# A conditioned attention layer with a routed feed-forward: two transposes of the attention stage moved from TensorE to VectorE's 32x32 blocks and transfers through memory

## The chip, the core and the metric

The kernel runs on one core of a Trainium2 chip. All data are fp32. The metric is the device time in microseconds of one execution. Three runs of the kernel before the change took 779.1, 781.33 and 787.7 us; the median, 781.33 us, is the time before. One more execution was profiled; the profile describes that one.

## What is computed

There are 16 sequences `x[b]` of 128 tokens, 256 wide, and for each a context of 128 tokens. Cut to what matters:

```python
z   = layernorm(layernorm(x)) * ln2_w + ln2_b
lat = z * (1 + cond) + cond                          # modulated, per sequence
kv_in = concat(layernorm(ctx) * ln1_w + ln1_b, lat)  # 256 tokens
q = lat @ Wq.T ;  k, v = split(kv_in @ Wkv.T)        # 16 heads of 64
x = x + (softmax(q @ k.T / 8) @ v) @ Wo.T
h = layernorm(x)                                     # "normed stream"
scores = h @ router                                  # 8 experts, the best one per token
x = x + shared_ffn(h) + routed_ffn(h, best expert)
```

Three places matter here. The two inputs of the attention, `ctx` and `x`, are normalised with tokens on partitions, and the projections need them with the 256 features on partitions: `kvT`. The result `h` of the second normalisation has tokens on partitions too, and the router and the shared feed-forward need it turned: `hT`. Both turns are what the change moves.

## The kernel before

Work goes in eight groups `g` of two sequences, b0 = 2g and b1 = 2g + 1. Attention runs in 32 **steps** `u`: one step is one sequence and half of its 16 heads, so a group has four: 2b0, 2b0+1, 2b1, 2b1+1. The order on every engine is the order in which the Python code emits instructions (a manual schedule), so each engine's queue is in program order, and a tile that is not yet free or not yet filled holds up all that is queued behind it.

`step(u, units, side, loads)` emits, in this order:

- `logits(u)` (L485): 8 products into two PSUM tiles `S`; then `keep_heads(u-2)` (L561, VectorE copies the heads of an earlier step out of PSUM);
- `maxima` of the first half (L497, VectorE), `exponents` of the first half (L504, ScalarE, 4 instructions), `maxima` of the second half;
- one **unit** from the list `units`; the `loads`; `normalise(u, 0)` (L514 a reciprocal on VectorE, L517 four multiplications on GpSimd); `exponents` of the second half;
- one unit; `normalise(u, 1)`; the first four of the `side` functions; one unit; the rest of `side`; all remaining units but one;
- `turn(u, n)` for both halves (L526: VectorE transposes 32x32 blocks of the probabilities into `px`; L530: SyncE's queue writes them to memory, `p_blocks`), `fetch(u)` (L538: SyncE's queue reads them back as `pT`, with keys on partitions); the last unit; `weigh(u-1)` (L550: probabilities times values for the step before).

A unit is a piece of TensorE work with the copy that takes its result out of PSUM: `k_unit` (L433, copied by ScalarE L441), `v_unit` (L452, copied by ScalarE L459), `q_unit` (L418, ScalarE L425), `finish` (L566, added to `xres` by VectorE L570), a piece of the shared feed-forward `hidden` (L149; SiLU on ScalarE L164, product on VectorE L165, in the last group only), and the two turns. All units share three PSUM buffers (`ps_m`, tag "mm"): a unit can start when the one three before it has been copied out. `S` has two buffers, `O` one.

The turns before the change:

- `inputs(g)`: statistics of four tiles (L314, L315), their variances (L320, L323), an inverse root by three Newton steps on tiny tiles (`newton`, L111 to L122), four normalisations in place or into `z` (L127); all as `side` of step 2b0+1, two groups ahead. Then `transpose([c])` for each half `c` of the features: four TensorE transposes against `ident` (L346, L347), and three VectorE instructions that apply weight and modulation while copying from PSUM into `kvT` (L348, L358). Half 0 is a unit of step 2b1, half 1 the first unit of the next group's step 2b0.
- `moe_inputs(g)`: the same for `h` of the group before: `x_rows` is written to memory (L581), statistics (L587, L588), variances (L593), its own Newton steps, normalisation and the write of `h_rows` (L604), as `side` of step 2b1; then in step 2b1+1 the unit `transpose` (L614: four TensorE transposes, L616: one VectorE copy into `hT`), and later the unit `choose` (L622: router products; L629).

The context tile `ctx` has one buffer, `xres` four, `kvT` two. `mwork` holds the tags "mid" (two buffers) and "xr" (three), which before the change only the feed-forward uses. After the last group come the rest of the shared feed-forward, the routing and 20 expert tiles; the change leaves them alone but for the place of one `choose`.

Of the kernel before, what the change touches and what calls it, by code (L numbers as in the profile page):

```python
# [9 lines left out]
F32 = mybir.dt.float32  # L10
# [7 lines left out]
P = 128  # L18
# [6 lines left out]
def resampler_attn__then__top1_moe_kernel(  # L25
# [100 lines left out]
    def normed(o, i, mr):  # L126
        nc.vector.tensor_scalar(o, i, mr[0], mr[1], ALU.subtract, ALU.mult)  # L127
# [118 lines left out]
    with ExitStack() as at:  # L246
# [53 lines left out]
        def inputs(g):  # L300

            st = {}

            def stats(i):
                if i == 0:
                    st["mv"] = small.tile([P, 4, 2], F32, tag="inmv", name=f"inmv_{g}")  # L310
                for k in (2 * i, 2 * i + 1):
                    t = (xres[g] if i == 0 else tokens[g])[:, k % 2, :]
                    s6 = small.tile([P, 6], F32, tag="inst", name=f"inst_{g}_{k}")
                    nc.vector.bn_stats(s6, t)  # L314
                    nc.vector.bn_aggr(st["mv"][:, k, :], s6)  # L315

            def variances():
                mv = st["mv"]
                v = small.tile([P, 4], F32, tag="inv", name=f"inv_{g}")
                nc.vector.tensor_scalar(  # L320
                    v[:, 0:2], mv[:, 0:2, 1], 1.0 + EPS, EPS * EPS, ALU.mult, ALU.add
                )
                nc.vector.tensor_scalar(v[:, 2:4], mv[:, 2:4, 1], EPS, None, ALU.add)  # L323
                st["newton"] = newton(small, v, 4, "in")

            def iterate(n):
                for _ in range(n):
                    st["r"] = next(st["newton"])

            def scale(i):  # L330
                if i == 0:
                    st["z"] = work.tile([P, 2, D], F32, tag="z", name=f"z_{g}", bufs=1)
                for k in (2 * i, 2 * i + 1):
                    t = (xres[g] if i == 0 else tokens[g])[:, k % 2, :]
                    o = (st["z"] if i == 0 else tokens[g])[:, k % 2, :]
                    normed(o, t, (st["mv"][:, k, 0:1], st["r"][:, k : k + 1]))

            def transpose(chunks):
                cs, z = tokens[g], st["z"]
                if chunks[0] == 0:  # L340
                    kvTs[g] = work.tile([P, DC, 2, 2, S], F32, tag="kvT", name=f"kvT_{g}")
                kvT = kvTs[g]
                for c in chunks:
                    pt = ps_m.tile([P, 2, 2, S], F32, tag="mm", name=f"kvt_{g}_{c}")
                    for i in range(2):
                        nc.tensor.transpose(pt[:, i, 0, :], cs[:, i, ts(c, P)], ident)  # L346
                        nc.tensor.transpose(pt[:, i, 1, :], z[:, i, ts(c, P)], ident)  # L347
                    nc.vector.tensor_scalar(  # L348
                        kvT[:, c, :, 0, :],
                        pt[:, :, 0, :],  # L350
                        vec[:, c, C_W1 : C_W1 + 1],
                        vec[:, c, C_B1 : C_B1 + 1],
                        ALU.mult,
                        ALU.add,
                    )
                    for i in range(2):
                        b = 2 * g + i
                        nc.vector.tensor_scalar(  # L358
                            kvT[:, c, i, 1, :],
                            pt[:, i, 1, :],  # L360
                            mod_w[:, c, b : b + 1],
                            mod_b[:, c, b : b + 1],
                            ALU.mult,
                            ALU.add,
                        )

            return (
                [lambda: stats(0), lambda: stats(1), variances]
                + [lambda: iterate(1)] * 3
                + [lambda: scale(0), lambda: scale(1)],  # L370
                transpose,
            )

        def first_inputs(i):
# [11 lines left out]
            nc.vector.tensor_scalar(  # L386
                v[:, 1:2], mv[:, 1, 1:2], 1.0 + EPS, EPS * EPS, ALU.mult, ALU.add
            )
            for r in newton(small, v, 2, "f"):
                pass  # L390
            z = work.tile([P, 2, D], F32, tag="z", name=f"fz_{i}", bufs=1)
            for k, t in enumerate(pair):
# [179 lines left out]
        def moe_inputs(g):  # L572

            b0 = 2 * g
            xr = xres[g]
            st = {}

            def stats():
                rows = slice(b0 * S, (b0 + 2) * S)
                keep_rows = s_rows if g == NG - 1 else x_rows  # L580
                nc.sync.dma_start(  # L581
                    out=keep_rows[rows, :].rearrange("(b p) d -> p b d", p=P), in_=xr
                )
                mv = small.tile([P, 2, 2], F32, tag="hmv", name=f"hmv_{g}")
                for i in range(2):
                    s6 = small.tile([P, 6], F32, tag="hst", name=f"hst_{g}_{i}")
                    nc.vector.bn_stats(s6, xr[:, i, :])  # L587
                    nc.vector.bn_aggr(mv[:, i, :], s6)  # L588
                st["mv"] = mv

            def variances():
                v = small.tile([P, 2], F32, tag="hv", name=f"hv_{g}")
                nc.vector.tensor_scalar(v, st["mv"][:, :, 1], EPS, None, ALU.add)  # L593
                st["newton"] = newton(small, v, 2, "h")

            def iterate():
                st["r"] = next(st["newton"])
# [1 line left out]
            def scale():  # L599
                st["h"] = work.tile([P, 2, D], F32, tag="h", name=f"h_{g}", bufs=1)  # L600
                for i in range(2):
                    normed(st["h"][:, i, :], xr[:, i, :], (st["mv"][:, i, 0:1], st["r"][:, i : i + 1]))
                rows = slice(b0 * S, (b0 + 2) * S)
                nc.sync.dma_start(  # L604
                    out=h_rows[rows, :].rearrange("(b p) d -> p b d", p=P), in_=st["h"]
                )
                xres.pop(g)
# [22 lines left out]

            return [stats, variances] + [iterate] * 3 + [scale], transpose, choose

        def step(u, units, side, loads=()):

# [2 lines left out]
            def aside(n):  # L639
                for f in side[:n]:  # L640
                    f()
                del side[:n]
# [18 lines left out]
            exponents(u, 1, ps[1], nm)  # L661
            unit()
            normalise(u, 1)
            aside(4)
            unit()
            aside(len(side))
            while len(units) > 1:
# [1 line left out]
            turn(u, 0)  # L669
            turn(u, 1)  # L670
            fetch(u)
            unit()
            if u > 0:
                weigh(u - 1)
# [17 lines left out]
            transpose(range(DC))  # L692
            load_tokens(2)

        late, in_rest = [], []
        for g in range(NG):
            b0, b1 = 2 * g, 2 * g + 1
            more = g + 1 < NG
            loads = [lambda: load_tokens(g + 2)] if 0 < g < NG - 2 else []
            q = [lambda j=j: q_unit(g + 1, j) for j in range(4)]  # L700
            k1 = [lambda j=j: k_unit(b1, j) for j in range(4)]
            v1 = [lambda j=j: v_unit(b1, j) for j in range(4)]
            k2 = [lambda j=j: k_unit(b1 + 1, j) for j in range(4)]
            v2 = [lambda j=j: v_unit(b1 + 1, j) for j in range(4)]
            wo_before = [lambda: finish(b0 - 1)] if g else []
            wo_first = [lambda: finish(b0)]
            if g > 0:
                late, h_transpose, choose = moe_inputs(g - 1)
                h_units = [h_transpose, choose]
            else:  # L710
                h_units = []
            new, in_transpose = inputs(g + 2) if g + 2 < NG else ([], None)
            if more:
                if g == 0:
                    step(0, k1 + [second_inputs] + q[:2], [])
                    load_shared()
                    v1 = [lambda j=j: v_unit(0, j) for j in range(1, 4)] + v1
                else:
                    step(2 * b0, in_rest + k1 + q[:2], [], loads)
                step(2 * b0 + 1, v1[:2] + wo_before + v1[2:], new)  # L720
                in_first = [lambda: in_transpose([0])] if in_transpose else []
                in_rest = [lambda f=in_transpose: f([1])] if in_transpose else []
                step(2 * b1, k2 + in_first + q[2:], late)
                step(2 * b1 + 1, v2[:1] + h_units[:1] + v2[1:2] + wo_first + h_units[1:] + v2[2:], [])
            else:

                sh = [shared_unit]
                step(2 * b0, k1 + sh * 2, [])
                step(2 * b0 + 1, wo_before + sh * 5, [])
                step(2 * b1, v1 + sh * 2, late)  # L730
                step(2 * b1 + 1, wo_first + sh + h_units[:1] + sh + h_units[1:] + sh, [])
        keep_heads(2 * B - 2)
        for j in range(NP // 2):
            shared_unit()
# [2 lines left out]
        keep_heads(2 * B - 1)  # L737
        shared_unit()
        finish(B - 1)
        late, h_transpose, choose = moe_inputs(NG - 1)  # L740
        for i, f in enumerate(late):
            f()
            if i % 2 == 1:
                shared_unit()
        shared_unit()
        h_transpose()
        shared_unit()
        choose()


    wexp = ctx.enter_context(tc.tile_pool(name="wexp", bufs=1))
# [425 lines left out]
```

## Time and profile before

| | |
|---|---|
| three runs | 779.1, 781.33, 787.7 us; median 781.33 |
| profiled execution, its own time | 778.67 us |
| span of its instructions | 776.8 us |
| granted TensorE clock | 1.0 |
| attention steps 2b0 to 2b1+1 of one middle group (S of 149.10 to S of 209.78) | 60.68 us |
| busy: TensorE, VectorE, ScalarE, GpSimd | 757.4, 412.6, 259.3, 313.0 us |
| mean DMA rate | 154 GB/s, 84,788 packets |

The span runs from the first to the last instruction of the program; the execution's own time is 1.9 us longer. In a line of the timeline the first number is the start in us from the span's start, the second the length, then engine, line, operation, written and read tiles; a bracket at the end says how long the engine had been idle and who released it. In a group line "x64 | 75.2, 1215" means 64 instructions, 75.2 us busy, 1215 ns each.

### The profile page before, as it was taken

Reading aid. Unit: us, or ns where it says so; the run is one execution under the profiler, and the core shown is the slowest. Engines: PE = TensorE matmul, PEld = TensorE weight load, DVE = VectorE, ACT = ScalarE, POOL = GpSimd, SP = SyncE. Lnnn points to the kernel's source line nnn. Section 1 sums busy time; section 2 is a strip of 40 time slices with the busy share of each in tenths; the row PEclk is TensorE's granted clock in tenths of the full one; section 3 lists DMA queues with packets and bytes.
Section 4 is the critical chain, followed back from the end, with each engine's and each line's share of the span. In section 5 each row is a group of like instructions: output and inputs, shape, how many; then the busy total and the mean of one; then the engine's idle time right before and its main releaser. Section 6 shows DMA issues by size and latency. Waiting matters only on the chain.

```text
span 776.8 us, 12221 instructions
## 1 busy us (share of the span) xinstructions
PE 757.4 (98%) x4156; PEld 587.0 (76%) x4156; DVE 412.6 (53%) x1000; ACT 259.3 (33%) x779; POOL 313.0 (40%) x366
## 2 busy tenths in 40 slices
PE   5999999999999999999999999999999999999997
PEld 4758768678677677687686777788888777787887
DVE  4475458558647647656744645635632354444532
ACT  2444533444354354344344455611311011010111
POOL 1363553464355345435544644521011234434331
PEclk9999999999999999999999999999999999999999
DMA  8075434633543553454345334532997334333332
GB/s 285 1 233 198 155 109 164 213 113 136 202 151 122 182 185 123 150 190 137 135 165 173 124 139 168 182 136 76 364 352 257 84 94 111 96 101 97 97 88 60
DMA packets 84788, 119.45 MB, mean 154 GB/s; under 512 B 10160, under 2 KB 68531, under 8 KB 84724
## 3 DMA queue, kind: packets, MB, share of 16 engines
q1 hardware_dynamic: 73380, 99.55, 37.8%
q0 software_dynamic: 4528, 13.18, 5.6%
q10 hardware_dynamic: 6816, 5.89, 2.5%
q8 instruction: 36, 0.59, 0.3%
q14 instruction: 28, 0.23, 0.1%
HBM read 68.78 MB, written 42.47 MB: 143 GB/s over the span
## 4 chain that ended last, share of the span: by engine, by line
PE 71%; DVE 15%; ACT 7%; issue 2%; DMA 2%; SPq 1%; POOL 0%; ACTq 0%; DVEq 0%; POOLq 0%
PE u L997 12%; PE pk L433 10%; PE pv L452 8%; PE p L149 8%; ACT pe L504 6%; PE yr L1046 6%; PE O L550 5%; PE pw L566 5%; PE S L485 5%; PE pq L418 5%; PE ys L179 5%; DVE px L526 3%; DVE nmx L497 2%; DVE ha L119 1%; DMA out_dram<-sg,table 1%
## 5 line engine op out<-in xcount | busy, mean ns | idle before, releaser
L517 POOL TENSOR_SCALAR pe<-pe,rs 128x256 f32<-128x256 f32 x256 | 230.9, 921 | 262.4 <-DVE rs L514 262.4
L504 ACT ACTIVATE pe<-S,nmx 128x256 f32<-128x256 f32 x256 | 118.4, 488 | 127.1 <-DVE nmx L497 127.1
L452 PE MATMUL pv<-wv,kvT 128*128 128x512 f32 x256 | 117.8, 601 | 0.2 <-ACT kT L441 0.2
L433 PE MATMUL pk<-kvT,wk 128*128 128x256 f32 x512 | 116.2, 386 | 0.4 <-DVE kvT L403 0.4
L433 PEld LDWEIGHTS pk<-kvT,wk 128*128 128x128 f32 x512 | 97.5, 193 | 16.7 <-issue 3.0
L526 DVE STREAM_TRANSPOSE px<-pe 128x512 f32<-128x512 f32 x128 | 81.4, 683 | 34.4 <-POOL pe L517 34.4
L997 PE MATMUL u<-w13s,xT 128*128 x320 | 98.0, 459 | 0.0
L452 PEld LDWEIGHTS pv<-wv,kvT 128*128 128x128 f32 x256 | 46.4, 190 | 50.3 <-issue 48.7
L997 PEld LDWEIGHTS u<-w13s,xT 128*128 128x128 f32 x320 | 59.4, 190 | 29.7
L497 DVE TENSOR_REDUCE nmx<-S 128x4 f32<-128x1024 f32 x64 | 75.2, 1215 | 12.3 <-PE S L485 12.3
L149 PE MATMUL p<-hT,ws 128*128 128x256 f32 x320 | 73.2, 381 | 0.5 <-DVE mid L165 0.5
L550 PEld LDWEIGHTS O<-pT,v 128*64 128x64 f32 x1024 | 55.2, 137 | 16.6 <-issue 14.6
L149 PEld LDWEIGHTS p<-hT,ws 128*128 128x128 f32 x320 | 60.1, 190 | 9.0 <-DVE mid L165 0.7
L485 PE MATMUL S<-kT,qT 64*128 64x256 f32 x512 | 63.9, 389 | 0.0
L1007 ACT ACTIVATE rsl<-u 128x352 f32<-128x352 f32 x40 | 18.4, 463 | 136.3 <-issue 67.8
L550 PE MATMUL O<-pT,v 128*64 128x128 f32 x1024 | 63.0, 276 | 0.0
L459 ACT COPY v<-pv 128x512 f32<-128x512 f32 x64 | 38.3, 599 | 73.0 <-PE pv L452 73.0
L566 PE MATMUL pw<-wo,oT 128*128 128x256 f32 x256 | 58.6, 382 | 4.0 <-ACT v L459 4.0
L566 PEld LDWEIGHTS pw<-wo,oT 128*128 128x128 f32 x256 | 48.1, 190 | 18.5 <-ACT v L459 9.8
L1008 DVE TENSOR_TENSOR body<-u,rsl 128x352 f32<-128x352 f32 x40 | 20.7, 524 | 74.1 <-issue 51.7
L418 PE MATMUL pq<-kvT,wq 128*128 128x256 f32 x256 | 58.1, 380 | 1.3 <-DVE kvT L358 1.3
L1046 PEld LDWEIGHTS yr<-wds,mT 128*128 128x128 f32 (+1 forms) x240 | 56.6, 309 | 2.0
(174 smaller groups left out, 810.6 us busy)
## 6 DMA issues: line engine op xcount, KB each, us to landing
p_blocks<-px SPq DMA_DIRECT2D x64, 512.0 KB
pT<-p_blocks SPq DMA_DIRECT2D x64, 512.0 KB
w13s<-in_w_dram SPq DMA_DIRECT2D x16, 704.0 KB
mT<-body SPq DMA_DIRECT2D x220, 24.0 KB
wds<-in_w_dram SPq DMA_DIRECT2D x8, 512.0 KB
mT<-body ACTq DMA_DIRECT2D x100, 24.0 KB
h_rows<-h SPq DMA_DIRECT2D x8, 256.0 KB
xres<-in_x_dram SPq DMA_DIRECT2D x7, 256.0 KB
```

The source lines that it names most:

```text
L149: nc.tensor.matmul(ps, lhsT=shared["w13"][:, c, ds(col, P)], rhs=hT[:, c, ts(t, TB)], start=(c == 0), stop=(c == DC - 1),)
L418: nc.tensor.matmul(pq[:, jj], lhsT=wq[:, c, ts(2 * j + jj, P)], rhs=kvTs[g][:, c, :, 1, :], start=(c == 0), stop=(c == DC - 1),)
L433: nc.tensor.matmul(pk[:, jj, :], lhsT=wk[:, c, ts(2 * j + jj, P)], rhs=kvTs[b // 2][:, c, b % 2].rearrange("p t s -> p (t s)"), start=(c = ...
L452: nc.tensor.matmul(pv, lhsT=kvTs[b // 2][:, c, b % 2, t, :], rhs=wv[:, c, ts(n, 512)], start=(c == 0), stop=(c == DC - 1),)
L485: nc.tensor.matmul(pl[:, r, j, :], lhsT=qTs[b // 2][rows, k, b % 2, :], rhs=kTs[b][rows, k, :], start=True, stop=True,)
L504: nc.scalar.activation(pes[u][:, h, :], pl[:, r, j, :], AF.Exp, bias=nmx[:, r, j : j + 1], accum_out=sums[u][:, h : h + 1],)
L517: nc.gpsimd.tensor_scalar(w, w, rs[:, i : i + 1], None, ALU.mult)
L526: nc.vector.transpose(px[:, :, t].rearrange("p j h q -> p h j q"), pes[u][:, ts(n, 4), ts(t, S)].rearrange("p h (j k) -> p h j k", k=BL),)
L550: nc.tensor.matmul(o[r * HD : (r + 1) * HD, j, :], lhsT=vs[b][:, t, ts(2 * (4 * half + j) + r, HD)], rhs=pTs[u][:, j // 2, :, t, 2 * (j % ...
L566: nc.tensor.matmul(pw, lhsT=outT[2 * b + k // 4][:, k % 4, :], rhs=wo[:, k, :], start=(k == 0), stop=(k == NP - 1))
L997: nc.tensor.matmul(pl[:, m, 0:FH], lhsT=xT[:, c, :], rhs=w13s[:, ds(e, 1), c, ds(m * F + n * FH, FH)].rearrange("p e f -> p (e f)"), start ...
L1046: nc.tensor.matmul(py, lhsT=mTs[j % 3][0:part, :, f], rhs=wds[0:part, ds(e, 1), f, :].rearrange("p e d -> p (e d)"), start=(f == 0), stop= ...
```

## The change

The inputs of group 0 (`first_inputs`) and of group 1 keep their TensorE transposes, and so does `h` of group 7. For groups 2 to 7 (`kvT`) and for `h` of groups 0 to 6 (`hT`) a new function `norms(gt, gh)` does both, gt = g + 2 and gh = g - 1:

- Statistics as before; the variances of both go into one tile of six columns, and one `newton` serves both.
- `t_turn`, `h_turn`: VectorE transposes 32x32 blocks within the tile (six instructions of 128x256), reading every fourth column; SyncE's queue writes the result to memory in 512-byte runs (two transfers of 256 KB for `kvT`, two of 128 KB for `hT`).
- `t_fetch`, `h_fetch`: SyncE's queue reads them back straight into `kvT` and `hT`, in runs of 32 elements (128 bytes).
- `modulate`: VectorE applies weight and modulation in place in `kvT`, as the last thing of a step's VectorE work.

The pieces are spread as follows. Step 2b0 gets the statistics of the inputs as `side` (before: step 2b0+1). Step 2b0+1 gets `h`'s statistics, the write of `x_rows` and the common inverse root, all after the third unit (`early=0`). Step 2b1 gets the normalisations, the block transposes and the writes. Step 2b1+1 gets the reads as `loads`, the loads of the next group but two, and `modulate` behind its `turn`. `choose` becomes the last unit of the next group's step 2b0. In the last group the shared feed-forward's pieces now stand ahead of `finish` in steps 2b0+1 and 2b1+1.

```diff
-            new, in_transpose = inputs(g + 2) if g + 2 < NG else ([], None)
...
-                    step(2 * b0, in_rest + k1 + q[:2], [], loads)
-                step(2 * b0 + 1, v1[:2] + wo_before + v1[2:], new)
-                in_first = [lambda: in_transpose([0])] if in_transpose else []
-                in_rest = [lambda f=in_transpose: f([1])] if in_transpose else []
-                step(2 * b1, k2 + in_first + q[2:], late)
-                step(2 * b1 + 1, v2[:1] + h_units[:1] + v2[1:2] + wo_first + h_units[1:] + v2[2:], [])
+            na, nb, nn, back, nd = norms(g + 2 if g + 2 < NG else None, g - 1 if g else None)
...
+                step(2 * b0, k1 + q[:2] + choose, na)
+            if g + 1 < NG:
+                step(2 * b0 + 1, v1[:2] + wo_before + v1[2:], nb, early=0 if g else 4)
+                step(2 * b1, k2 + q[2:], nn)
+                ahead = [lambda: load_tokens(g + 3)] if g + 3 < NG else []
+                step(2 * b1 + 1, v2[:2] + wo_first + v2[2:], [], back + ahead, behind=nd)
             else:
                 sh = [shared_unit]
-                step(2 * b0, k1 + sh * 2, [])
-                step(2 * b0 + 1, wo_before + sh * 5, [])
-                step(2 * b1, v1 + sh * 2, late)
-                step(2 * b1 + 1, wo_first + sh + h_units[:1] + sh + h_units[1:] + sh, [])
+                step(2 * b0, k1 + sh * 2 + choose, [])
+                step(2 * b0 + 1, sh * 2 + wo_before + sh * 3, nb, early=0)
+                step(2 * b1, v1 + sh * 2, nn)
+                step(2 * b1 + 1, sh * 2 + wo_first + sh, [], back, behind=nd)
```

The new functions, cut to their core:

```python
def iterate():
    for st["r"] in newton(small, var(), nt + nh, f"j{nt + nh}"): pass

def t_turn():
    rows = mwork.tile([P, FC + 1, TB], F32, tag="mid", name=f"tx_{gt}")
    ...
    for m in range(4):
        nc.vector.transpose(
            px[:, :, m],
            (st["z"] if m % 2 else tokens[gt])[:, m // 2, :].rearrange(
                "p (c k j) -> p c j k", c=DC, k=BL))
    for c in range(DC):
        nc.sync.dma_start(
            out=t_blocks[gt % 2][c].rearrange("m i k j q -> (i k) m (j q)"),
            in_=px[:, c].rearrange("p m j q -> p m (j q)"))

def t_fetch():
    kvTs[gt] = work.tile([P, DC, 2, 2, S], F32, tag="kvT", name=f"kvT_{gt}")
    for c in range(DC):
        nc.sync.dma_start(
            out=kvTs[gt][:, c].rearrange("p b t (i q) -> p (b t i) q", q=BL),
            in_=t_blocks[gt % 2][c].rearrange("m i k j q -> (k j) (m i) q"))

def modulate(c):
    kvT = kvTs[gt][:, c]
    scaled(kvT[:, :, 0, :], vec[:, c, C_W1 : C_W1 + 1], vec[:, c, C_B1 : C_B1 + 1])
    for i in range(2):
        b = 2 * gt + i
        scaled(kvT[:, i, 1, :], mod_w[:, c, b : b + 1], mod_b[:, c, b : b + 1])
```

`scaled` is one VectorE multiply-and-add in place. `h_turn` and `h_fetch` are the same with two tiles instead of four and `hT` as the target, `h_turn` into a tile of tag "xr".

## The prediction, made before the changed kernel was run

> **What bounds the kernel now.** I read the page first: TensorE is busy nearly all of the span, and most of the chain that ended last is TensorE.
>
> ```profile
> PE 757.4 (98%) x4156; PEld 587.0 (76%) x4156; DVE 412.6 (53%) x1000; ACT 259.3 (33%) x779; POOL 313.0 (40%) x366
> ...
> PE 71%; DVE 15%; ACT 7%; issue 2%; DMA 2%; SPq 1%; POOL 0%; ACTq 0%; DVEq 0%; POOLq 0%
> ```
>
> A busy TensorE need not be a bound one (ends of matmuls are modelled), and 22% of the chain is VectorE and ScalarE. So next the timeline of TensorE over two steps of a middle group, 2b1 and 2b1+1 of g = 2:
>
> ```profile
> 178.21 2.00 PE L485 MATMUL S<-kT,qT 64*128 64x256 f32 x16
> 180.14 7.17 PE L433 MATMUL pk<-kvT,wk 128*128 128x256 f32 x32
> 187.15 0.27 PE L346 MATMUL kvt<-ident,ctx 128*128 128x128 f32 x1
> 187.26 0.27 PE L347 MATMUL kvt<-ident,z 128*128 128x128 f32 x1
> 187.37 0.27 PE L346 MATMUL kvt<-ident,ctx 128*128 128x128 f32 x1
> 187.48 0.27 PE L347 MATMUL kvt<-ident,z 128*128 128x128 f32 x1
> 187.59 3.62 PE L418 MATMUL pq<-kvT,wq 128*128 128x256 f32 x16
> ...
> 193.03 2.00 PE L485 MATMUL S<-kT,qT 64*128 64x256 f32 x16
> 194.96 1.98 PE L452 MATMUL pv<-wv,kvT 128*128 128x512 f32 x4
> 196.78 0.60 PE L614 MATMUL ph<-ident,h 128*128 128x128 f32 x4
> 197.22 1.88 PE L452 MATMUL pv<-wv,kvT 128*128 128x512 f32 x4
> 199.91 3.72 PE L566 MATMUL pw<-wo,oT 128*128 128x256 f32 x16 [0.81 <-ACT v L459]
> 203.46 0.95 PE L622 MATMUL pr<-wr,hT 128*128 128x8 f32 x8
> ```
>
> Starts follow each other without a hole but for one, 0.81 us. So TensorE sets the pace, and what is taken off its queue shortens the step, as long as the other engines keep up. The list of waits of TensorE says how often they don't (us in total, times, longest):
>
> ```profile
> PE pw L566 <- ACT v L459: 4.0, 5, 0.8
> PE pq L418 <- DVE kvT L358: 1.3, 2, 0.9
> PE pr L622 <- DVE hT L616: 0.9, 1, 0.9
> ```
>
> The wait of 0.8 is the chain's VectorE share. VectorE's timeline shows the cause:
>
> ```profile
> 180.69 2.34 DVE L497 TENSOR_REDUCE nmx<-S 128x4 f32<-128x1024 f32 x2
> ...
> 196.15 2.34 DVE L497 TENSOR_REDUCE nmx<-S 128x4 f32<-128x1024 f32 x2
> ```
>
> On time, the maxima start 1.18 us after S starts (163.87 to 165.05 a step earlier). Here they start at 180.76 and 196.22 by the chain, 1.4 and 2.0 us late, since side work ran ahead of them. ScalarE's copy of the first `pv` ends 3.6 us after the maxima start; `pw` needs that buffer because `ph` took one of the three.
>
> **What is removed.** By start-to-start distance, four `kvt` transposes hold TensorE for 0.49 us at the head of step 2b0 (151.02 to 151.52) and 0.44 us above, four `ph` for 0.44 us. Six groups of inputs: 6 x 0.93 = 5.6 us. Seven of `h`: 7 x 0.44 = 3.1 us. The rows' 273 to 285 ns each would give twice that, but they overlap. Sum 8.7 us. The mean of a TensorE step is 15.2 us, so this is small.
>
> With `ph` gone, `pv`, `pv`, `pw` fill three buffers and the fourth unit asks for the first buffer 3.45 us later: the 0.81 us waits go, 5 x 0.81 = 4.0 us. In the last group `pr` no longer stands behind the copy of `hT`: 0.9 us. The wait of `pq` for L358 is group 1's and stays. `choose` moves but costs TensorE the same 0.8 us. Gain so far 13.6 us.
>
> **VectorE, step by step.** Gone per group: the copies L348 and L358 (0.45 + 0.64 us by starts, twice), L616 (0.6), one Newton chain (about 3 us). New: six block transposes of 128x256 and `modulate`.
>
> ```profile
> L526 DVE STREAM_TRANSPOSE px<-pe 128x512 f32<-128x512 f32 x128 | 81.4, 683 | 34.4 <-POOL pe L517 34.4
> L1016 DVE STREAM_TRANSPOSE body<-body 128x512 f32<-128x512 f32 x20 | 22.3, 1113 | 0.7
> ```
>
> The first reads and writes runs of 32: 0.60 us from start to start for 512 columns, so 0.33 for 256. The second writes every sixth element and takes nearly double. The new ones read every fourth element, 16 bytes apart. The Trainium skill (page "SBUF — State Buffer", the note on cachelines) says that SBUF lines are 16 bytes and that an access which crosses to a new line each time pays; by it the new transposes are of the second kind, 0.57 us. Six cost 2.0 us by the first row, 3.4 by the rule and the second; I take the second. `modulate` is 0.33 + 2 x 0.2 us twice (normalisations L127 run at 0.33), 1.5 us.
>
> Now the lateness of the maxima. Step 2b0+1: `pw` ends 8.8 us after S starts, its addition at 9.25; statistics 1.07, variances 0.37, Newton 2.9 (the four-column one took 2.84), `px` 2.5, `oT` 0.6: maxima at 16.6 against 15.4 on time, 1.3 to 2.0 us late. Queued behind it are `kT`'s copies; `pk` number four asks for the first copy 7.1 us after S, the copy ends at 1.2 + 3.6: it may be 2.3 us late. No stall, 0.3 to 1 us to spare. Step 2b1: normalisations 2.05, six transposes 2.0 to 3.4, where before 6.8 us of side work stood: lateness 0 to 2.3 afterwards, allowed 4 in step 2b1+1. There GpSimd sets the end of `px` (12.0 us after the maxima, 196.15 to 208.1), then `modulate`: lateness is kept, and step 2b0 absorbs it. So I cost VectorE at nothing; its cover is this slack.
>
> **The transfers.** Added per group on SyncE's queue: writes of 512 + 256 KB, reads of the same in 128-byte packets, 8 issues at 0.33 to 0.37 us. `p_blocks` of step 2b1 is queued behind the writes, which fall into a stretch (189 to 193) in which the transfer records are empty: nothing. `x_rows` (0.5 us of issue) moves one step earlier, the token loads of the next group stand behind the reads and are wanted 8 us after the next S: nothing; GpSimd's queue gets and loses nothing. On SyncE's queue the reads wait for their writes, done some 10 us before; behind them stands `p_blocks` of the same step, issued only after 10 us more. `hT` (1.8 us of packets) is asked for by `pr` at the end of the next step: nothing. The reads stand behind `pT` of step 2b1, and `modulate` waits for them with the next maxima behind it. No row has 128 bytes. In the trace's transfer records a 160-byte packet (`vec`) takes 14 ns, 1024 bytes (`pT`) 46, 4096 bytes 159: a line through these gives 13 ns for 128, 27 for 512. `kvT` needs 256 packets per engine: 3.6 us at 14 ns, 11.8 at 46. The skill (page "DMA: Bandwidth & Descriptors", Specifications) wants at least 512 bytes for line rate and says that smaller ones are read-modify-written; this speaks against the change: at a 512-byte price it is 6.9 us. Counted from S of step 2b1+1: `px` of step 2b1 ends at about 1, `pT` has landed 6.9 later (195.65 to 202.5 before), so `kvT` by 12 at 14 ns; VectorE asks at 13.2. Until it is 2.3 us late TensorE does not feel it: the bound is 7.1 us of reading, 28 ns a packet. I take 14 ns, `vec` being nearest in size: nothing, also by the rule, barely.
>
> **What the last group gives back.** Four activation tables more are loaded (1.28 us each), because a SiLU now stands between the two halves of `exponents` in steps 2b0+1 and 2b1+1. In step 2b0+1 the second SiLU comes at 10.8 instead of about 7 us after S; its product frees a PSUM buffer at 11.2, asked for at 10.6: 0.6 us. Then statistics and Newton (5 us) stand on VectorE ahead of the products of the shared pieces and of `px`; the next maxima are 3.9 us late, and with `pv` first, TensorE waits for the copies of `pv` 1.7 + 0.6 us. In step 2b1+1 the second reciprocal waits for the second SiLU, GpSimd ends at 15.6 after S, `px` at 16.9, `pT` lands 6.9 later at 23.8, and `weigh` asks at 22.2: 1.6 us; with 0.2 us for `ys` the sum is 4.7 us (0, if VectorE slips these in, to 7).
>
> **The sum.** 8.7 + 4.0 + 0.9 - 4.7 = 8.9 us. Span 776.8 - 8.9 = 767.9, the profiled time 778.67 - 8.9 = 769.8. The profiled run is 2.7 us under the median; on the median, 781.33 - 8.9 = 772.4 us.
>
> **Rivals.** (a) *The give-back does not happen*: all 13.6 us come, 767.7 us. For: VectorE has holes in these steps; against: its queue is in order. (b) *128-byte reads cost as much as the 1024-byte ones*, 46 ns: `modulate` is 4.7 us beyond the bound in each of six groups, 28 us, and the time is 772.4 + 28 = 800, slower than before; from 28 ns on it eats gain, at 36 ns all of it. For: the size rule; against: `vec`. (c) *VectorE is the real pace*: side work only moves, the 22% of the chain stay, waits of 0.8 us reappear before `pk` in step 2b1 as fast as transposes go: 13.6 - 4.0 - 4.7 - 6 x 0.8 = about 0, 781 us. Against it, the step's slack above.
>
> **How the numbers follow.** My forecast has 0.64, 766 to 778 by itself; (a) 0.14, (b) 0.12, (c) 0.10. About 1%, 7.8 us, is what can be told from no change: below 773.5 counts as faster. The forecast lies on that edge: 0.39 of its 0.64 is faster. Faster 0.39 + 0.14 = 0.53, same 0.25 + 0.10 = 0.35, slower 0.12. The range, 763 to 786, takes in (a), (c) and the lower part of (b).
>
> **What would show it.** Right: 48 + 28 transposes fewer and no `ph`; `pw` without its 0.8 us; VectorE's L727 with no idle time before it; new TensorE waits only after the last group's `finish`. Wrong: idle time before L727 that ends with the landing of `kvT`, packets of 128 bytes above 28 ns, block transposes above 0.6 us, or waits before `pk` in every group.

## The result and the profile after

Four runs of the changed kernel took 771.84, 771.90, 771.98 and 775.41 us, median 771.94; the kernel before took 780.22 us (median of four). The ratio is 0.990, 95% interval 0.987 to 0.993. The forecast was 772.4 us, range 763 to 786. The same kernel was measured once more, beside the experiments below: 769.40 us (six runs) against 780.07 (thirteen), ratio 0.985 (0.982 to 0.988). So the gain is 8 to 11 us. The profiled execution is the one of 775.41 us. From its page, the line of the engines and the chain of work that ended last:

```profile
span 773.7 us, 12112 instructions
...
PE 752.0 (97%) x4080; PEld 581.5 (75%) x4080; DVE 407.6 (53%) x971; ACT 263.8 (34%) x783; POOL 315.1 (41%) x366
...
PE 3%; SPq 2%; DMA 0%; issue 0%; DVE 0%
```

There are 76 matmuls fewer (48 + 28), as the diff says. VectorE's busy sum is 5 us lower, although its work is another. The chain can't be set beside that of before: it was followed back only through the last few per cent, and says nothing of the attention stage. The timeline of TensorE does, for the steps 2b1 and 2b1+1 of g = 2, the ones that the prediction showed:

```profile
176.19 2.00 PE L485 MATMUL S<-kT,qT 64*128 64x256 f32 x16
178.12 7.17 PE L433 MATMUL pk<-kvT,wk 128*128 128x256 f32 x32
185.13 3.62 PE L418 MATMUL pq<-kvT,wq 128*128 128x256 f32 x16
188.68 1.97 PE L550 MATMUL O<-pT,v 128*64 128x128 f32 x32
190.57 2.00 PE L485 MATMUL S<-kT,qT 64*128 64x256 f32 x16
192.50 3.70 PE L452 MATMUL pv<-wv,kvT 128*128 128x512 f32 x8
196.04 3.62 PE L566 MATMUL pw<-wo,oT 128*128 128x256 f32 x16
199.49 3.60 PE L452 MATMUL pv<-wv,kvT 128*128 128x512 f32 x8
```

No `kvt`, no `ph`, and no bracket with an idle time: `pw` follows at once. Summed over the four steps of that group, first after, then before (window; busy time and count of PE, PEld, DVE, ACT, POOL; TensorE clock; DMA share; GB/s):

```profile
146.68:204.92 58.24, 58.24 (x363) 43.88 (x361) 36.90 (x85) 25.77 (x84) 29.16 (x32) 1.00 0.61 192
```

```profile
149.10:209.78 60.68, 59.88 (x374) 44.84 (x372) 38.04 (x91) 25.83 (x84) 28.86 (x32) 1.00 0.45 157
```

The group is 2.44 us shorter, and TensorE is busy in all of it. The DMA share rose from 0.45 to 0.61, and no wait of TensorE comes of it here. VectorE in the same two steps:

```profile
178.56 2.34 DVE L497 TENSOR_REDUCE nmx<-S 128x4 f32<-128x1024 f32 x2
...
185.86 0.63 DVE L705 STREAM_TRANSPOSE tx<-ctx 128x256 f32<-128x256 f32 x1
186.43 0.59 DVE L705 STREAM_TRANSPOSE tx<-z 128x256 f32<-128x256 f32 x1
186.94 0.60 DVE L705 STREAM_TRANSPOSE tx<-ctx 128x256 f32<-128x256 f32 x1
...
192.76 2.33 DVE L497 TENSOR_REDUCE nmx<-S 128x4 f32<-128x1024 f32 x2
...
203.56 1.30 DVE L526 STREAM_TRANSPOSE px<-pe 128x512 f32<-128x512 f32 x2 [2.23 <-POOL pe L517]
204.78 0.37 DVE L727 TENSOR_SCALAR kvT<-kvT,vec 128x256 f32<-128x256 f32 x1
```

A block transpose takes 0.54 us from start to start (185.86 to 186.94 for two). "On time" is again 1.18 us after S: the maxima start 1.2 us late (178.56 against 176.19 + 1.18) and 1.0 us late (192.76). L727 (`modulate`) follows `px` with no idle time: the blocks had landed. What TensorE still waits for, where it did not before:

```profile
PE yr L1185 <- DMA mT<-body: 3.1, 2, 2.1
PE O L550 <- DMA pT<-p_blocks: 1.3, 1, 1.3
...
PE pr L149 <- DVE mid L165: 0.8, 1, 0.8
...
PE ys L179 <- DVE mid L165: 0.4, 1, 0.4
PE pv L452 <- ACT v L459: 0.4, 1, 0.4
PE p L149 <- ACT v L459: 0.3, 1, 0.3
```

All but the first are in the last group. `yr` is in the expert stage, and its waits come some 200 us after the last unit that the change moves. To tell the parts apart I cut each trace at the first `S` of steps 0 and 29 (S29 is that of the last group's step 2b0+1) and at the first expert product `u`; medians are those of the runs, and each ratio is to runs of the kernel before taken beside them (their medians, 779.6 to 780.2 us, differ little):

| kernel | median us | ratio to before (95%) | S0 to S29 | S29 to u | u to end |
|---|---|---|---|---|---|
| before (profile of 778.67 us) | 780.07 | 1 | 437.32 | 135.19 | 176.2 |
| changed, first measurement | 771.94 | 0.990 (0.987-0.993) | 423.72 | 137.98 | 182.6 |
| changed, again | 769.40 | 0.985 (0.982-0.988) | 423.71 | 137.67 | 179.7 |
| last group in the old order | 765.85 | 0.981 (0.978-0.984) | 423.71 | 134.23 | 178.6 |
| before, `ph` late | 774.43 | 0.992 (0.989-0.995) | 431.95 | 135.20 | 177.1 |
| changed, `h` on TensorE | 775.49 | 0.994 (0.991-0.996) | 426.35 | 141.03 | 177.2 |
| the same, last group old | 769.35 | 0.988 (0.986-0.990) | 426.34 | 134.47 | 177.0 |
| changed, reads doubled | 775.91 | 0.995 (0.994-0.997) | 428.59 | 138.61 | 177.8 |
| changed, reads tripled | 804.09 | 1.030 (1.026-1.033) | 458.06 | 138.04 | 179.5 |
| changed, second Newton | 779.42 | 0.999 (0.997-1.002) | 432.55 | 137.63 | 183.8 |
| changed, `mT` nine to seven | 768.98 | 0.986 (0.983-0.988) | 423.71 | 138.08 | 177.5 |
| last step alone changed | 768.09 | 0.986 (0.984-0.987) | 423.72 | 136.34 | 178.4 |

The first two stretches hold all that the change touches, and repeat to 0.5 us where that part of the kernel is the same. The last one doesn't repeat: it takes 176 to 184 us with the same instructions.

### The profile page after: what moved, and what is told of

Same layout as the page of the kernel before. It is cut to its first block, busy times and chain, and to the rows that moved or that the text cites. A ratio compares the mean times of both kernels' runs of the same rounds, so it can differ in the third digit from the quotient of the medians.

```text
span 773.7 us, 12112 instructions
## 1 busy us (share of the span) xinstructions
PE 752.0 (97%) x4080; PEld 581.5 (75%) x4080; DVE 407.6 (53%) x971; ACT 263.8 (34%) x783; POOL 315.1 (41%) x366
## 5 line engine op out<-in xcount | busy, mean ns | idle before, releaser
L433 PE MATMUL pk<-kvT,wk 128*128 128x256 f32 x512 | 117.9, 389 | 0.6 <-DVE kvT L403 0.6
L1185 PE MATMUL yr<-wds,mT 128*128 (+1 forms) x240 | 59.0, 397 | 3.1 <-DMA mT<-body 3.1
L514 DVE RECIPROCAL rs<-sums 128x4 f32<-128x4 f32 x64 | 11.4, 177 | 91.8 <-ACT pe L504 91.8
```

What stands on the lines that cost most here:

```text
L433: nc.tensor.matmul(pk[:, jj, :], lhsT=wk[:, c, ts(2 * j + jj, P)], rhs=kvTs[b // 2][:, c, b % 2].rearrange("p t s -> p (t s)"), start=(c = ...
L1185: nc.tensor.matmul(py, lhsT=mTs[j % 3][0:part, :, f], rhs=wds[0:part, ds(e, 1), f, :].rearrange("p e d -> p (e d)"), start=(f == 0), stop= ...
```

## The experiments

The theory to test: TensorE sets the pace, so the gain is the transposes taken from it, at their start-to-start distance, and the wait of `pw`; VectorE and the transfers are covered by slack of a few us; the last group's order gives part of it back. The rivals: the transposes were hidden and only the wait counted; VectorE is the pace; what was given back comes from the way through memory.

**The changed kernel again**, nothing edited: where do the 2 us between the attention stage's gain and the first measurement go?

> The changed kernel, nothing edited. The attention stage of the profiled execution gained 9.6 us from the start to the first expert product (10.8 us counted from the first S), but the times only 8.3 us, and that execution lost 3.1 us in three waits of TensorE for mT (an expert's gathered tokens) at the tail. Theory A (the lost 3 us are the tail's: SyncE issues the mT transfers for 7.1 of a tile's 7.6 us, so that a hiccup is not made up): an execution without those waits ends at 770 to 772 us and shows yr waits for mT under 1.2 us in all. Theory B (the loss is in the start, where this execution began its attention 1.25 us later): S of step 0 starts again at 29.3 us instead of 28.1. Ratio to the kernel before 0.988 to 0.992 by both.

769.40 us. The stage from S0 to `u` gains 572.51 - 561.38 = 11.1 us, the medians 780.07 - 769.40 = 10.7. Theory B falls: this execution reaches its first S at 28.09 us, as the kernel before did, and over all the traces that start lies between 27.2 and 29.3 us. A is only half met: this execution ends at 770.93 us and still waits 1.9 us for `mT`. What is left is mostly scatter of the expert stage, from one execution to the next; the times of the kernel before scatter too (778.3 to 786.2 us in the thirteen runs).

The traces say what that scatter is made of. From the first `u` to TensorE's last matmul, less TensorE's idle time there, ten of the twelve traces take 172.2 to 172.9 us. The idle time, nearly all of it `yr` waiting for `mT` where it is long, is 0 in the kernel before, 1.9 us in this run, 3.1 in the first measurement and 4.1 with the second Newton chain below. The end behind the last matmul takes 3.9 to 5.3 us. And in the two traces with the longest single waits, the matmuls themselves take some 2 us more. Here is `yr` behind its wait in the first measurement, with the window that follows it, and then the same in this run (the last three columns of a window are TensorE's granted clock, DMA share and GB/s):

```profile
748.78 4.64 PE L1185 MATMUL yr<-wds,mT 128*128 x12 [2.10 <-DMA mT<-body]
748.78:752.78 4.00, 4.00 (x11) 3.29 (x12) 0.42 (x1) 0.39 (x1) 0.88 (x1) 0.58 0.32 82
```

```profile
745.40 3.02 PE L1185 MATMUL yr<-wds,mT 128*128 x12 [1.92 <-DMA mT<-body]
745.40:749.40 4.00, 4.00 (x18) 3.84 (x19) 0.85 (x2) 0.38 (x1) 0.87 (x2) 1.00 0.31 80
```

Behind 2.10 us of waiting the granted clock was 0.58 over the next 4 us and twelve `yr` took 4.64 us; behind 1.92 us it stayed at 1.00 and they took 3.02. Why `mT` lands late in one execution and not in another is not shown.

**The last group in the old order.** The other groups stay changed.

```diff
-                step(2 * b0 + 1, sh * 2 + wo_before + sh * 3, nb, early=0)
-                step(2 * b1, v1 + sh * 2, nn)
-                step(2 * b1 + 1, sh * 2 + wo_first + sh, [], back, behind=nd)
+                step(2 * b0 + 1, wo_before + sh * 5, [])
+                step(2 * b1, v1 + sh * 2, nb + nn)
+                step(2 * b1 + 1, wo_first + sh * 3, [], back, behind=nd)
```

> The last group (g = 7) alone goes back to the order of before: shared pieces behind the finish units, statistics and normalisation of h together in step 2b1. Theory (the give-back of the last group comes from that order: SiLUs between exponents, statistics and Newton ahead of the products): the waits for mid L165, ACT v L459 and pT in this group (0.8 + 0.4 + 0.3 + 1.3 + 0.4 us) go, and the time is 3 to 4 us below the changed kernel, about 768 us. Rival (the give-back comes from the way of h through memory, which this kernel keeps): within 1 us of the changed kernel.

765.85 us, 3.55 below the changed kernel of the same session; S29 to `u` 3.4 us shorter. Of the last group's waits one is left:

```profile
506.41 1.09 PE L550 MATMUL O<-pT,v 128*64 128x128 f32 x16 [0.35 <-DMA pT<-p_blocks]
```

So it is the new order of the last group that gives the time back, not the way of `h` through memory, which this kernel keeps. This version is the best of those run: 0.981 of before.

**The kernel before, with `ph` behind `pw`.** All transposes stay on TensorE. The router's unit (`choose`, `pr`), which needs the copy of `ph`, goes back by one place too.

```diff
-                step(2 * b1 + 1, v2[:1] + h_units[:1] + v2[1:2] + wo_first + h_units[1:] + v2[2:], [])
+                step(2 * b1 + 1, v2[:2] + wo_first + h_units[:1] + v2[2:3] + h_units[1:] + v2[3:], [])
```

> The kernel before, with only the unit that turns h (ph) moved in step 2b1+1 from between the two v units to behind the first finish (pw). Theory (the 0.81 us waits of pw come from ph holding one of three PSUM buffers while the maxima are late): the five waits go, 4 to 5 us less than the kernel before, 775 to 776 us, with all transposes still on TensorE. Rival (VectorE is the real pace in these steps, the wait only moves to pr or the next pk): within 1 us of before.

774.43 us: 5.6 us from moving `ph` by two places and `pr` by one. TensorE in step 2b1+1 of g = 2:

```profile
194.79 3.70 PE L452 MATMUL pv<-wv,kvT 128*128 128x512 f32 x8
198.33 3.62 PE L566 MATMUL pw<-wo,oT 128*128 128x256 f32 x16
201.78 0.60 PE L614 MATMUL ph<-ident,h 128*128 128x128 f32 x4
202.22 1.88 PE L452 MATMUL pv<-wv,kvT 128*128 128x512 f32 x4
203.94 0.95 PE L622 MATMUL pr<-wr,hT 128*128 128x8 f32 x8
```

No idle time, nor is it passed on to `pr` or to the next step. The buffer that `ph` held was the cause, and VectorE isn't the pace here. The step went from 16.75 to 15.68 us: 1.07, not the 0.81 of the bracket. The parts of it can be read from starts. Four `pv` take 1.71 us from their start to the next unit's where nothing waits (202.22 to 203.94 above). In the kernel before they would have let `pw` start at 197.22 + 1.71 = 198.93; it started at 199.91, 0.98 later. The bracket counts from the (modelled) end of the last matmul, which otherwise overlaps its successor by 0.17. And the waiting `pw` took 3.55 us to the next start (199.91 to 203.46), where it takes 3.45 above (198.33 to 201.78): 0.1 more. The sum is 1.08.

**`h` on TensorE again**, with four `ph` and a VectorE copy; the inputs keep the new way.

```diff
-            h = [[], [h_stats, h_variances], [h_scale, h_turn], [h_fetch], []] if nh else [[]] * 5
+            h = [[], [h_stats, h_variances], [h_scale], [], []] if nh else [[]] * 5
...
-                step(2 * b1 + 1, v2[:2] + wo_first + v2[2:], [], back + ahead, behind=nd)
+                step(2 * b1 + 1, v2[:1] + ht + v2[1:2] + wo_first + v2[2:], [], back + ahead, behind=nd)
...
-                step(2 * b1 + 1, sh * 2 + wo_first + sh, [], back, behind=nd)
+                step(2 * b1 + 1, sh * 2 + wo_first + ht + sh, [], back, behind=nd)
```

> The changed kernel with h turned by TensorE again (four ph and the copy L616 in step 2b1+1, between the v units as before; no blocks and no memory for h); the inputs keep the new way. Theory A (a transpose costs its start-to-start distance, and the wait of pw needs maxima that are 2 us late, which they no longer are): 7 x 0.44 = 3.1 us above the changed kernel, no wait of pw. Theory B (the place of ph between the v units is enough for the wait): 3.1 + 7 x 0.8 = 8.7 us above. Theory C (the transposes were hidden, all gain was the wait): 0.

775.49 us, 6.1 above the changed kernel, between A and B. The steps tell where. S0 to S29 is 2.64 us longer = 6 x 0.44, and `pw` follows `ph` and `pv` at once, in the old place. The rows are TensorE's, with the maxima of the same step (VectorE) as the second one:

```profile
190.04 2.00 PE L485 MATMUL S<-kT,qT 64*128 64x256 f32 x16
191.22 2.36 DVE L497 TENSOR_REDUCE nmx<-S 128x4 f32<-128x1024 f32 x2
...
193.79 0.60 PE L749 MATMUL ph<-ident,h 128*128 128x128 f32 x4
194.23 1.88 PE L452 MATMUL pv<-wv,kvT 128*128 128x512 f32 x4
195.94 3.62 PE L566 MATMUL pw<-wo,oT 128*128 128x256 f32 x16
...
499.05 2.07 PE L149 MATMUL pr<-hT,ws 128*128 128x256 f32 x4 [2.73 <-DVE mid L165]
```

So C falls (the transposes weren't hidden), and B too: `ph` stands in its old place, and no `pw` waits. The maxima start on time here (191.22 is 190.04 + 1.18), since VectorE has no block transposes of `h` in this run; they were on time in group 6 of the kernel before too, which had no wait either, and 1.9 us late in its five groups that had one. At 1.0 us, the lateness of the changed kernel, no run has `ph` in that place. The rest, 3.4 us, lies in the last group, most of it in the last line: I had put `ph` ahead of a piece of the shared feed-forward, which waits for a product on VectorE. The clock was lower behind that wait too:

```profile
499.05:502.15 3.10, 3.10 (x14) 2.27 (x16) 2.15 (x5) 0.38 (x1) 2.90 (x4) 0.50 0.04 16
```

To take that wait away, the same was run with the last group in the old order (`wo_first + sh + ht + sh * 2`):

> The run with h on TensorE once more, but with the last group in the order of before, so that its ph stands where it stood and not ahead of a product of the shared feed-forward. In the earlier run the middle groups had lost 0.44 us each, as theory A there said, and the last group 3.4 us. Expected against the run with the last group's old order and h through memory (765.85 us): 7 x 0.44 = 3.1 us more, about 769 us, no wait of pr for mid L165. Rival (ph costs more than its start-to-start distance also here): 772 or more.

769.35 us, 3.5 above the run with the old order and `h` through memory; S0 to `u` 2.9 us longer. The start-to-start price holds.

**The reads doubled and tripled.** An extra read of the same blocks, into a tile that nobody uses, goes ahead of each read of `kvT` (one tile, then two):

```diff
+                idle = [mwork.tile([P, FC + 1, TB], F32, tag="mid", name=f"idle_{gt}_{k}") for k in range(1)]
                 for c in range(DC):
+                    for t in idle:
+                        nc.sync.dma_start(
+                            out=t[:, 2 * c : 2 * c + 2].rearrange("p b (m q) -> p (b m) q", q=BL),
+                            in_=t_blocks[gt % 2][c].rearrange("m i k j q -> (k j) (m i) q"),
+                        )
```

> The changed kernel, with each read of kvT's blocks preceded by one more of the same blocks into an unused tile: 256 packets of 128 bytes per engine more, 3.3 us at 13 ns, so about 6.9 us of reading for kvT where 7.1 us was the bound. In the changed kernel kvT landed about 12.3 us after S of step 2b1+1 and VectorE asked for it at 14.2. Theory (the reads have slack, up to 7.1 us of reading): VectorE waits 1.5 to 3 us ahead of L727, TensorE does not feel it, 0 to 3 us above the changed kernel (about 770). Rival (no slack behind the reads: p_blocks and pT stand on the same queue and everything shifts): 6 x 3.3 = 20 us above.

> As the run before, with two more reads for each: 512 packets per engine more, 6.7 us, 10.2 us of reading for kvT, 3 us beyond the bound. This is what packets of 128 bytes at 39 ns would have cost. Theory of the bound: VectorE waits 5 to 6 us ahead of L727 and TensorE loses 3 to 4 us in each of six groups: 18 to 25 us above the changed kernel, about 790, slower than before. Rival (VectorE and TensorE have more slack than estimated): under 8 us above.

775.91 and 804.09 us, 6.5 and 34.7 above the changed kernel. Both miss their theory on the same side: there is slack, but less than estimated. VectorE with the reads doubled, g = 2 (the first row is `modulate` of the second half of `kvT`):

```profile
207.73 0.41 DVE L733 TENSOR_SCALAR kvT<-kvT,vec 128x256 f32<-128x256 f32 x1 [1.67 <-DMA kvT<-t_blocks]
...
209.17 2.35 DVE L497 TENSOR_REDUCE nmx<-S 128x4 f32<-128x1024 f32 x2
```

`S` of this step 2b0 starts at 205.32, so the maxima are 2.7 us late, and the step is 1.1 us longer: about 1.6 us of lateness is free. The second half of `kvT` landed 16.8 us after S of step 2b1+1, where `modulate` asks for it at 15.1. The landing in the changed kernel can only be bounded, since nothing waits for it there and the reads of `hT` in the same queue have packets of the same size: the first 4,096 such packets, as many as `kvT` has, were through 12.3 us after S in the second measurement (12.6 in the first), the last of both reads at 14.4 us. With the reads doubled that last packet ended at 17.2 us, with the reads tripled at 21.2. So 256 packets per engine more took 2.8 us and 512 took 6.8 (2.8 to 3.9 and 6.0 to 7.6 in the five groups with both reads), 11 to 15 ns each, about what the record of one lasts (13 ns). The second half, which asked at 15.1, waited 1.7 us for 2.8 us of added reading: some 1.1 us was to spare in this group. With the reads tripled `kvT` lands at 20.4 us, and TensorE in step 2b0 of g = 3 reads:

```profile
212.94 5.45 PE L433 MATMUL pk<-kvT,wk 128*128 128x256 f32 x24
222.26 3.78 PE L433 MATMUL pk<-kvT,wk 128*128 128x256 f32 x8 [3.87 <-ACT kT L441]
225.84 4.58 PE L418 MATMUL pq<-kvT,wq 128*128 128x256 f32 x16
```

The wait is 3.9 us, but the step is 6.9 us longer. The same 8 `pk` take 1.99 us in other runs and the 16 `pq` 3.62. The windows of these rows, with the granted clock third from the right:

```profile
211.01:222.26 11.25, 7.38 (x42) 5.94 (x40) 4.89 (x10) 2.46 (x10) 0.22 (x1) 0.94 0.95 225
222.26:226.04 3.78, 3.78 (x9) 3.06 (x10) 1.86 (x8) 2.75 (x10) 3.78 (x5) 0.50 0.84 250
226.04:230.45 4.41, 4.41 (x20) 3.74 (x18) 2.86 (x8) 1.18 (x2) 3.23 (x4) 0.80 0.36 143
```

After the wait the granted clock is 0.50, then 0.80. By the rows above, that is 1.8 + 1.0 us on top of the 3.9.

**A second Newton chain** in step 2b0+1, with a result that nobody uses: VectorE's time for two separate inverse roots, both in this step (before the change they stood in two steps).

```diff
+                if nt and nh:
+                    for st["r0"] in newton(small, var(), nt + nh, "jx"):
+                        pass
```

> The changed kernel with a second chain of Newton steps on six columns in step 2b0+1, whose result is not used (in six groups): what two separate inverse roots cost VectorE, 2.6 to 3 us more ahead of the maxima of step 2b1. They started 1.0 to 1.2 us late in the changed kernel and may be 2.3 us late by the estimate. Theory (the slack is about 2.3 us): 3.6 to 4 us late, TensorE loses 1.3 to 1.8 us in each of six groups, 8 to 11 us above the changed kernel. Rival (VectorE off the path has slack enough): within 1.5 us.

779.42 us, 10.0 above the changed kernel (S0 to `u`: 8.8). The theory holds, though the chain fell into five groups and not six. VectorE and TensorE in step 2b1 of g = 2, S at 176.05:

```profile
180.58 2.34 DVE L497 TENSOR_REDUCE nmx<-S 128x4 f32<-128x1024 f32 x2
```

```profile
184.34 1.99 PE L433 MATMUL pk<-kvT,wk 128*128 128x256 f32 x8 [0.91 <-ACT kT L441]
186.65 3.72 PE L418 MATMUL pq<-kvT,wq 128*128 128x256 f32 x16 [0.32 <-ACT kT L441]
```

The maxima are 3.35 us late, and the step is 1.77 us longer (16.15 against 14.38), in five groups. Again about 1.6 us is free. The two brackets sum to 1.23, and 0.27 comes on top for each. So two roots in this step would take nearly the whole gain of the change (the ratio is 0.999), though VectorE is busy 53% of the time. Whether two roots in two steps would do so was not run.

**The expert stage's transfers split nine to seven** between SyncE's and ScalarE's queues (`n < 9` for `n < 11` at L1166).

> The changed kernel, with the sixteen mT transfers of an expert tile split nine to seven between SyncE's and ScalarE's queues in place of eleven to five. Theory (SyncE's issues, 7.1 of a tile's 7.6 us, make the tail late after any hiccup; the span from the first expert product to the end was 176.2 to 182.6 us in the profiles so far): yr never waits for mT, that stretch is 176 us in each profile, and the time is 1 to 3 us below the changed kernel, about 767. Rival (the stretch varies for another reason): within 0.7 us; or slower, if two more issues on ScalarE's queue delay the SiLUs.

768.98 us, 0.4 below: the rival. `yr` doesn't wait for `mT` in this profile, and its last stretch is 177.5 us, but the medians differ by less than the runs of either scatter. The split isn't shown to help: one trace without the wait is no proof that it is gone.

**The last group's steps 2b0+1 and 2b1 alone in the old order** (the first two lines of the first diff above).

> The changed kernel, of the last group only steps 2b0+1 and 2b1 in the old order (shared pieces behind finish, statistics and Newton in step 2b1); step 2b1+1 stays changed. Each idle time of TensorE has cost its length and 0.26 us more so far. Theory (the give-back has two causes): the waits of pr for mid (0.8), pv (0.6) and p (0.3) for ScalarE's copies of v go, 1.7 + 3 x 0.26 = 2.5 us below the changed kernel, about 767; those of ys (0.4) and O for pT (0.8 to 1.3) stay. Rival (all of it comes from the last step): within 0.7 us of the changed kernel (769.4).

768.09 us, 1.3 below the changed kernel, between the two. The steps 29 and 30 lose their 2.5 us of waits (29.59 instead of 32.10 us together), but half comes back in the step that was left as it is:

```profile
494.05 5.45 PE L179 MATMUL ys<-wsd,mid 128*128 128x256 f32 x24 [1.51 <-DVE mid L165]
```

`ys` waited 0.41 us in the changed kernel and 1.51 here. So the give-back has two causes, the order of steps 2b0+1 and 2b1 and that of step 2b1+1, and the waits of one hid part of the other's.

## Why the prediction was right, and which of its terms were off

The time came out within 0.5 us of the forecast in the first measurement and 3 us under it in the second. The mechanism was right: TensorE's queue got shorter, the wait went with the buffer, and VectorE's new work was covered. That the first came so close is in part luck: the attention stage gained some 2 us more than forecast, and in the profiled execution the start and the expert stage lost more than that. Term by term, from the stretches of the traces (those of the last group from the second measurement):

- *Transposes of the inputs*, said 5.6 us: the two places are 0.44 us and 0.39 (said 0.49) in six groups, 5.0 us. Those of `h`, said 3.1 us: 2.64 for six and 0.44 for the seventh, confirmed by undoing it (2.9 us in the trace, 3.5 in the medians).
- *The wait of `pw`*, said 4.0 us: five times 1.07, 5.4 us, shown alone in the kernel before. It was mis-sized, since a bracket's idle time was taken where the transposes were priced by starts.
- *`choose` moves at the same price*: 0.90 us in its old step, 0.79 in the new, 0.7 us gained over six groups and not foreseen. `pr` behind `hT`: the 0.9 us went.
- *VectorE costs nothing*: true, but with less room than said. Lateness was 1.2 us in step 2b1 (said 1.3 to 2.0), 1.0 in 2b1+1 (said 0 to 2.3). What is allowed ahead of the `pk` units is 1.6 us by two experiments, not 2.3. The block transposes took 0.54 us, so the choice of 0.57 by the cacheline rule (the Trainium skill, "SBUF — State Buffer", the note on cachelines) over the 0.33 of the nearest row was right; no run reads the same blocks without the stride.
- *Transfers cost nothing*: true. The packets of 128 bytes took 11 to 13 ns in nearly all records (13 in 96%), so the line through the neighbouring sizes was right. The Trainium skill ("DMA: Bandwidth & Descriptors", Specifications) puts transfers under 512 bytes below line rate, and the small packets are slower per byte: 13 ns for 128 bytes, 159 for 4096. But the packets of 512 bytes took 27 to 32 ns, so 128 bytes show no price of read-modify-writing beyond that line. `kvT` was through between 12.3 and 14.4 us after S (said 12), and VectorE asked at 14.2 (said 13.2). The bound, 7.1 us of reading, was too wide: with twice the packets, about 6.9 us by that working, 1.1 to 1.4 us were lost in four of six groups.
- *The last group gives back*, said 4.7 us: step 29 is 1.06 us longer than without its wait (said 0.6), step 30 1.45 (said 2.3), then `ys` and `pT` 0.41 + 0.79, and 0.26 for each (said 1.8). Sum 4.2; undoing the order brought 3.4 to 3.6 of it.

Measured: 5.0 + 3.1 + 5.4 + 0.7 + 0.9 - 4.2 = 10.9, where the trace has 11.1 from S0 to `u`; forecast 8.9. The first measurement showed 8.3. In its profiled execution the stage gained 10.8 us, the start cost 1.3 us more and the expert stage 6.4; of its other executions there is no trace. Rival (a) is refuted by the waits and by undoing them. Rival (b) had the right consequence for a price that did not occur: tripled reads, as if a packet took 39 ns, cost 35 us, twice what the bound gives for them (17). Its working also says that 36 ns eat all of the gain; by its own bound 34 do (8.9 us over six groups of 256 packets, on top of 28), and by the doubled reads 26 ns already eat 6.5 us. Rival (c) fails in the group windows, but it was nearer than its chance said: one more Newton chain, which puts the maxima 2.2 us later in five groups, turns the change into none.

What stays open: why `mT` lands late in some executions. The waits of `yr` for it and the lower clock behind the longest of them account for most of the spread from 176 to 184 us in the expert stage, but relieving SyncE's queue did not shorten the median.

## What to carry to other kernels

On an engine that sets the pace, price everything by the distance between starts, waits too; and before moving work to another engine, look for a small unit that holds a shared buffer across a wait, since here moving `ph` by two places gave half of the gain at no cost. Slack of an engine off the path is counted at the one instruction that the path asks for next (here 1.6 us for the maxima), not by its share of busy time, and it can be measured by adding a known piece of work. Regrouping side work that pays in the middle of a loop should be tried apart on its last turn, where other units take the place of those that covered it: here it gave back 3.5 us. And a single long wait costs more than its length when the clock is lower behind it.

## What the runs showed of the hardware

- A hole (idle time) of 0.3 to 0.9 us in TensorE's timeline costs 0.26 to 0.27 us more than its bracket says. For the 0.81 us of `pw`, that is the overlap with the matmul ahead (0.17, by the profile's modelled ends) and a slower restart (0.1).
- A hole of 3.9 us cost 6.9: the granted clock was 0.50 in the next 3.8 us and 0.80 in the 4.4 after them. Shorter holes lowered the clock too: behind 2.10 us it was 0.58 over the next 4.0 us, behind 2.73 us 0.50 over the next 3.1. Behind 1.92 us it stayed at 1.00. The Trainium skill ("TensorE: Matmul & The Clock Gate", Part 1) says that the array falls to half its clock after an idle window of about 3.4 us; here less was enough, and the measurement decides.
- Packets of 128 bytes from memory to SBUF took 13 ns each, and all 16 engines together moved up to about 1,600 of them in a microsecond. Over a whole read, an extra packet per engine cost 11 to 15 ns.
